# A Mamba-2 layer with a small mixture of experts: dt's logarithm in PSUM, sums of squares by transposes, six banks and new prices in the planner

## The chip, the core and the metric

The kernel runs on one core of a Trainium2 chip. TensorE (PE) multiplies, VectorE (DVE), ScalarE (ACT) and GpSimd (POOL) work on the elements, and SyncE (SP) issues the DMAs. The metric is the time on the device in microseconds (us) for one launch; less is better. All data are fp32.

## The reference

A sequence of 1024 tokens with 512 features is normalised (layernorm without weights). Two branches take the result, and both are added to the input.

The first is a Mamba-2 layer with 128 heads of 64 channels, state size 128, 8 groups, and chunks of 128 tokens:

```python
proj = einsum('bsd,ed->bse', x, in_proj_w)       # 18560 rows: gate 8192, hBC 10240, dt 128
hBC = silu(conv1d(hBC, width 4, per channel) + conv_b)
hs, B, C = split(hBC)                            # 8192, 8 x 128, 8 x 128
dt = clip(softplus(dt + dt_bias), 0, 100)
A_dt = dt * -exp(A_log);  A_cum = cumsum over a chunk
Y_diag = C B^T * exp(segsum(A_dt)) @ (hs * dt)   # inside a chunk
states = B^T @ (hs * dt * exp(A_last - A_cum))   # handed from chunk to chunk
Y_off = C @ previous state * exp(A_cum)
y = (Y_diag + Y_off + hs * D) * silu(gate)
out = rmsnorm in 8 groups of 1024 (y) * norm_w @ out_proj_w.T
```

The second is a linear layer of 512 x 512 plus LoRA experts of rank 16: softmax over 8 experts, the best two, weights renormalised, scaled by 2.

## The kernel before

**Precision.** A wide product of fp32 matrices is made of three products of fp32r halves: high x high, high x low, low x high. ScalarE rounds the high half, POOL (or VectorE) subtracts to get the low half (`split`, L311). Some products (y, yo, cb, the old sums of squares) are plain fp32 and appear as two records each in the trace.

**The start.** x is loaded in eight blocks, normalised, transposed on TensorE (xT) and split into XH and XL (L352 to L391). The dt rows are projected first (pp_dt, two halves of 512 tokens, L407). Softplus is relu(v) + log(1 + exp(-|v|)): ScalarE writes |v| to `dtu` and relu(v) to `dtv` in SBUF, then the exponential in place in `dtu`; VectorE evaluates a polynomial of degree 10 for the logarithm (L433 to L438: one scaling and nine multiply-adds per half), adds, clips, multiplies by A and scans (`ac`, L445). `dtv`, `ac` and the decay are transposed (tt_dt, tt_As, tt_dec). The router and the FFN (`ffn`, L482) run in between; the FFN's products are pf0 to pf7.

**The middle.** For each unit u of 4 heads (32 units): two blocks of the gate and two of hs are projected by `block` (L639, 12 products of 512 columns per half, bank pp_r), hs goes through the convolution (ScalarE the first tap, VectorE three, L658 and L667) and silu; hs is transposed (hT, L749) and multiplied by dt (xdt); decay gives xf, split into xdh and xdl (L757 to L766); 21 products ps of 256 columns make the chunk states (L775), which VectorE chains (st, L782 to L787); yo (L808) is the part from earlier chunks, y (L819) the part inside a chunk, with the matrix L that ScalarE (L731, L733) and VectorE (L735) build from a broadcast load of A_cum. VectorE evacuates them (tt L811, yt L823), POOL adds and multiplies by the gate (L826, L829), and the result is stored in DRAM (g_d). Every fourth unit, `group` projects B and C and makes cb (L679).

**The end.** For each group g of 1024 channels and each block z of 128 tokens, the gated values come back (gr), are split into gh and gl, and are multiplied by the split output weights (po, 24 products of 512 columns, L891). For the norm, ScalarE squares in place, VectorE sums over the eight channel blocks (sq, L883), and TensorE sums over the partitions: a product of sq with a column of ones gives one number per token (vp, L902), for two blocks z at a time. ScalarE takes the root (L904), VectorE the reciprocal, and po times it is added to acc (L910). With the last group acc is stored.

**What sets the order.** The program's instructions are recorded as `op`s with an engine, a planned duration, an urgency and the buffers they take. `Plan.run` (L123) then replays planned times and, whenever an engine is free, takes the ready op with the smallest urgency whose buffers are there. The resulting order is fixed in each engine's queue; at run time semaphores alone decide when an instruction starts. PSUM is a pool of 8 banks, and `BANKS` caps how many of each kind may live: mm (wide accumulators, also bt and cb), ts (transposes, ps, vp) and yy (y and yo). An op that is marked `long` is of the wide sort on TensorE:

```python
                    if o.table and o.table != table:
                        urge += URGE["switch"]
                    if e == "PE" and o.long != long:
                        urge += URGE["turn"]
```

A wide op after one that isn't long also costs `TURN` in the plan (L196 to L199). ps isn't marked long here.

## Time and profile before

| | |
|---|---|
| median of 3 runs (lowest to highest) | 1666.13 us (1664.14 to 1667.02) |
| profiled execution, its own time | 1664.26 us |
| its span, first to last instruction | 1662.5 us |
| mean granted TensorE clock | 0.997 |
| busy share of PE, DVE, ACT, POOL | 98%, 78%, 76%, 53% |
| ACT table loads | 176 |
| wide projections pp_r | 3456 products |
| output projection po | 1536 products |
| y, yo, ps, hT records | 2048, 896, 672, 512 |
| vp records | 128, 16.3 us busy |

In the lines shown below, a row of the timeline reads: start and length in us, engine, line of the kernel, operation, output and inputs (buffer numbers left out), shapes, how many were merged, and in brackets the idle time before it and what ended it. A row of the table of stretches reads: from and to, length, then busy us and count of instructions for PE, PEld (weight loads), DVE, ACT and POOL, the granted TensorE clock, the DMA share and GB/s. A row of a tile's page under "its engine sat idle before it" names who ended the wait, the us in total and how many times. Rows of neighbouring products overlap, since a product's length includes its way through the array; the distance between two starts is what one product costs.

### The profile page before, as it was taken

The page shows a single profiled execution, that of the slowest core. Times are in us where ns is not written, and L with a number is a line of the kernel's source. Part 1 is how long each engine was busy: PE and PEld are TensorE (multiplying, and loading weights), DVE is VectorE, ACT ScalarE, POOL GpSimd, SP SyncE. Part 2 cuts the span into 40 slices and gives each one's busy share as a digit, 9 for nine tenths or more (in the row PEclk, how much of TensorE's full clock was granted, in tenths as well). Part 3 has the DMA queues.
Part 4 walks back from the last instruction along what each step waited for, and adds up shares of the span by engine and source line. Part 5 has one row for each costly group of instructions (what it writes and reads, how often), then busy time and mean ns, then how long its engine had stood idle before and what let it go on. Part 6 is the DMA issues. An engine that isn't in the chain of part 4 may idle for free.

```text
span 1662.5 us, 27030 instructions
## 1 busy us (share of the span) xinstructions
PE 1635.5 (98%) x9732; PEld 1363.3 (82%) x9732; DVE 1298.8 (78%) x2205; ACT 1268.0 (76%) x2262; POOL 881.2 (53%) x769
## 2 busy tenths in 40 slices
PE   7999999999999999999999999999999999999998
PEld 5688888888888888888888888888887788888887
DVE  7249978878787888787777878877779987787774
ACT  4836999897998889899979979898999444444441
POOL 4017866875866687677758766875776300000000
PEclk9999999999999999999999999999999999999999
DMA  4542644534444355344434444545454755544522
GB/s 140 178 145 76 194 134 141 172 127 149 132 129 148 113 157 164 130 130 162 143 118 144 128 136 129 174 143 158 128 175 143 212 152 152 137 124 122 151 67 72
DMA packets 142903, 234.07 MB, mean 141 GB/s; under 512 B 11312, under 2 KB 76976, under 8 KB 142768
## 3 DMA queue, kind: packets, MB, share of 16 engines
q1 hardware_dynamic: 142768, 232.33, 45.6%
q8 instruction: 77, 1.26, 0.3%
q14 instruction: 58, 0.48, 0.1%
HBM read 193.49 MB, written 38.80 MB: 140 GB/s over the span
## 4 chain that ended last, share of the span: by engine, by line
PE 80%; DVE 5%; ACT 3%; issue 2%; POOL 1%; DMA 1%; SPq 0%; DVEq 0%; ACTq 0%; POOLq 0%
PE pp_r L401 38%; PE po L891 20%; PE y L819 6%; PE yo L808 6%; PE ps L775 5%; PE hT L749 3%; DVE h L667 2%; DVE L L735 1%; PE cb L705 1%; DVE owl L866 1%; PE vp L902 1%; ACT g L651 1%; POOL xdl L764 1%; ACT xdh L762 1%; DVE sq L883 0%
## 5 line engine op out<-in xcount | busy, mean ns | idle before, releaser
L401 PE MATMUL pp_r<-xh,wh 128*128 128x512 f32 x1152 | 465.2, 404 | 0.0
L401 PE MATMUL pp_r<-xl,wh 128*128 128x512 f32 x1152 | 450.8, 391 | 0.0
L401 PE MATMUL pp_r<-xh,wl 128*128 128x512 f32 x1152 | 450.8, 391 | 0.0
L731 ACT ACTIVATE L<-L,As 128x128 f32<-128x128 f32 x1024 | 316.6, 391 | 0.9 <-DMA L<-acum_d 0.8
L667 DVE SCALAR_TENSOR_TENSOR h<-pp_r,cw,h 128x512 f32<-128x512 f32 (+2 forms) x384 | 287.2, 748 | 36.5 <-ACT h L658 27.5
L313 POOL TENSOR_TENSOR wl<-wr,wh 128x512 fp32r<-128x512 f32 x144 | 187.3, 1310 | 169.3 <-ACT wh L312 157.2
L826 POOL TENSOR_TENSOR yt<-yt,tt 128x384 f32<-128x384 f32 (+1 forms) x128 | 180.2, 1410 | 153.6 <-DVE tt L811 92.8
L401 PEld LDWEIGHTS pp_r<-xh,wh 128*128 128x128 f32 x1152 | 217.1, 188 | 46.7 <-issue 6.2
L401 PEld LDWEIGHTS pp_r<-xh,wl 128*128 128x128 f32 x1152 | 216.5, 188 | 47.2
L401 PEld LDWEIGHTS pp_r<-xl,wh 128*128 128x128 f32 x1152 | 217.3, 189 | 40.2 <-issue 0.2
L735 DVE TENSOR_TENSOR L<-L,cbm 128x1024 f32<-128x1024 f32 x128 | 189.5, 1487 | 35.3 <-ACT L L733 34.9
L829 POOL TENSOR_TENSOR g<-yt,g 128x512 f32<-128x512 f32 x128 | 181.7, 1422 | 5.8
L764 POOL TENSOR_TENSOR xdl<-xf,xdh 128x512 fp32r<-128x512 f32 (+1 forms) x128 | 149.6, 1187 | 56.2 <-ACT xdh L762 56.2
L757 POOL TENSOR_TENSOR xf<-xdt,dec 128x512 f32<-128x512 f32 (+1 forms) x128 | 152.6, 1208 | 37.2 <-DVE xdt L751 37.1
L786 DVE SCALAR_TENSOR_TENSOR st<-st,eA,ps 128x64 f32<-128x64 f32 x768 | 150.3, 275 | 1.1
L883 DVE TENSOR_REDUCE sq<-gr 128x128 f32<-128x1024 f32 x64 | 128.4, 2007 | 18.0 <-ACT gr L882 17.2
L658 ACT ACTIVATE h<-pp_r,cb,cw 128x512 f32<-128x512 f32 (+1 forms) x128 | 98.5, 770 | 57.5 <-PE pp_r L401 56.9
L819 PE MATMUL y<-L,xdt 128*64 128x128 f32 x2048 | 135.6, 278 | 1.6 <-DVE L L735 1.0
L733 ACT ACTIVATE L<-L 128x1024 f32<-128x1024 f32 x128 | 135.4, 1058 | 1.4
L819 PEld LDWEIGHTS y<-L,xdt 128*64 128x64 f32 x2048 | 110.0, 136 | 28.3 <-issue 9.4
L891 PE MATMUL po<-owh,gh 128*128 128x512 f32 x512 | 131.8, 397 | 0.0
L882 ACT ACTIVATE gr<-gr 128x1024 f32<-128x1024 f32 x64 | 67.7, 1058 | 80.8 <-DVE gl L880 80.3
(174 smaller groups left out, 2809.3 us busy)
## 6 DMA issues: line engine op xcount, KB each, us to landing
L<-acum_d SPq DMA_DIRECT2D x128, 512.0 KB, 5.7
wr<-in_w SPq DMA_DIRECT2D x144, 256.0 KB, 3.0
g_d<-g SPq DMA_DIRECT2D x64, 512.0 KB, 3.0
gr<-g_d SPq DMA_DIRECT2D x64, 512.0 KB, 6.9
e<-exp_d SPq DMA_DIRECT2D x128, 224.0 KB, 4.5
ow<-out_w SPq DMA_DIRECT2D x64, 256.0 KB, 3.1
x<-x SPq DMA_DIRECT2D x8, 256.0 KB, 4.7
xa<-x SPq DMA_DIRECT2D x8, 256.0 KB, 3.2
```

Of the source, the lines that this page charges most:

```text
L313: op("POOL", dur[1], lambda: pool.tensor_tensor(lo(), raw(), f32(hi()), ALU.subtract), r=[raw, hi], w=[lo], urge=urge, port=True)
L401: pe.matmul(acc(), a[:, k, :], b[:, k, halves(half)], start=n == 0, stop=n == 11)
L667: dve.scalar_tensor_tensor(d, acc()[:, :n], cw[:, ci, k:k + 1], d, ALU.mult, ALU.add)
L731: act.activation(L()[:, z, :], L()[:, z, :], AF.Relu, bias=As()[:, z, h:h + 1], scale=-1.0)
L735: op("DVE", 1.14, lambda L=L: dve.tensor_tensor(L(), L(), gr.cbm(), ALU.mult), r=[gr.cbm], w=[L], urge=at("Lm") + 0.05 * a, port=True)
L757: op("POOL", 1.0 if n == 4 else 0.8, lambda xf=xf, j=j, b=b, zs=zs, n=n: pool.tensor_tensor(xf().rearrange("p z (a c) -> p z a c", a=2), x ...
L764: op("POOL", 1.24 if n == 4 else 0.96, lambda xf=xf, zs=zs, cols=cols: pool.tensor_tensor(xdl()[:, zs, cols], xf(), f32(xdh()[:, zs, cols] ...
L786: dve.scalar_tensor_tensor(st()[:, z, c], st()[:, z - 1, c], eA()[:, 4 * u + a, z:z + 1], pt()[:, z % 2, c], ALU.mult, ALU.add)
L819: pe.matmul(yp()[64 * a:64 * a + 64, zsl(z4)], xdt[j]()[:, z, 64 * a:64 * a + 64], M[2 * j + a]()[:, z, :], start=True, stop=True)
L826: op("POOL", 1.3 if n == 4 else 1.0, lambda yt=yt, tt=tt, part=part: pool.tensor_tensor(yt()[:, part], yt()[:, part], tt()[:, part], ALU.a ...
L829: op("POOL", 1.3, lambda yt=yt, j=j, hf=hf: pool.tensor_tensor(gate[j]()[:, halves(hf)], yt(), gate[j]()[:, halves(hf)], ALU.mult), r=[yt] ...
L891: pe.matmul(po(), a()[:, b, :], wts[g, b // per][k]()[:, b % per, :], start=n == 0, stop=n == 23)
```

## The change

- **dt.** The exponential stays in PSUM: ScalarE writes |v| and then exp(-|v|) in place into the accumulator pp_dt, and VectorE's polynomial reads it there. Its instructions are no longer planned on the SBUF port shared with POOL (`port=True` goes), so the plan doesn't keep them apart from POOL's.
- **Sums of squares.** sq of four blocks z (two in the last group) share one tile. TensorE transposes each of them (128 columns, one record) into one bank, and VectorE reduces along the tokens' rows in PSUM; then the root on ScalarE and the reciprocal for all four at once. Four po accumulators wait for it instead of two.
- **Banks.** mm may hold six banks instead of five.
- **Prices.** Going from wide to narrow on TensorE costs an urgency of 0.065, from narrow to wide 0.135 (before 0.018 both ways), and `TURN` is 0.13 instead of 0.09. ps counts as long. Most other urgencies have new values.
- **Loads.** The planned landing times of the eight loads of x differ, and the dt weights are loaded after the sixth instead of the fourth. Some planned durations are new.

```diff
--- before.py
+++ after.py
@@ -41,7 +41,8 @@
 SWITCH = 1.3
-TURN = 0.09
-URGE = dict(w=-0.906, part=-0.044, proj=0, evac=-0.05, silu=0, group=-0.136, hT=0.273, xdt=0.663, xf=1.191,
-            split=0.55, ps=0.69, st=0.536, Ll=0.1, Lr=1.008, Le=0.296, Lm=1.16, el=0.3, yo=0.952, tt=0.642, y=0.92,
-            yt=0.737, out=0.8, switch=0.3, turn=0.018, c0=32.2, c=0.022, ffn=-3.656, early=-3.5, w0=31)
-BANKS = dict(mm=5, ts=3, yy=3)
+TURN = 0.13
+URGE = dict(w=-0.813, part=-0.179, proj=0, evac=0.099, silu=-0.096, group=-0.136, hT=0.272, xdt=0.765, xf=1.065,
+            split=0.327, ps=0.69, st=0.495, Ll=0.114, Lr=1.681, Le=0.456, Lm=1.16, el=0.441, yo=1.177, tt=0.256,
+            y=1.1, yt=0.811, out=0.8, switch=0.345, short=0.065, long=0.135, c0=32.207, c=0.032, ffn=-2.955,
+            early=-3.189, w0=31)
+BANKS = dict(mm=6, ts=3, yy=3)
 
@@ -151,3 +152,3 @@
                     if e == "PE" and o.long != long:
-                        urge += URGE["turn"]
+                        urge += URGE["short" if long else "long"]
                     if best is not None and (best_urge, best.n) <= (urge, o.n):
@@ -248,4 +249,2 @@
                        channel_multiplier=-1)
-    ones = ctile([P, 1], "ones")
-    pool.memset(ones, 1.0)
     eps_t = ctile([P, 1], "eps_t")
@@ -277,3 +276,3 @@
     K |= {n: Kind(small, c) for n, c in dict(wr=3, wh=3, wl=3, y=2, tt=2, xf=2).items()}
-    K |= {n: Kind(small, c, late=True) for n, c in dict(acc=8, sq=3, ow_r=4).items()}
+    K |= {n: Kind(small, c, late=True) for n, c in dict(acc=8, sq=2, ow_r=4).items()}
     banks = Pool("banks", 8, HALF, psum)
@@ -333,7 +332,8 @@
         for i in range(2):
-            dma(lambda xt=xt, i=i: xt()[:, i, :], lambda z=2 * j + i: x[zsl(z), :], 3.0, w=[(xt, 1 << i)],
+            dma(lambda xt=xt, i=i: xt()[:, i, :], lambda z=2 * j + i: x[zsl(z), :],
+                (2.7, 2.9, 4.3, 4.6, 4.8, 5.0, 5.3, 5.5)[2 * j + i], w=[(xt, 1 << i)],
                 urge=-8.0 + 0.01 * j)
         xts.append(xt)
-        if j == 1:
-            dma(wdt[0], lambda: in_w[144], 3.0, w=[wdt[0]], urge=-7.985)
+        if j == 2:
+            dma(wdt[0], lambda: in_w[144], 5.2, w=[wdt[0]], urge=-7.975)
 
@@ -368,6 +368,6 @@
         for i in range(2):
-            op("DVE", 0.8, stats(i), r=[(xt, 1 << i)], w=[(sc, 1 << i)], urge=ur)
+            op("DVE", 0.87, stats(i), r=[(xt, 1 << i)], w=[(sc, 1 << i)], urge=ur)
         op("ACT", 0.2, lambda mv=mv, rs=rs: act.activation(rs, mv[:, 1:4:2], AF.Sqrt, bias=eps_t), r=[sc], w=[sc],
            urge=ur, table="sqrt")
-        op("DVE", 0.25, scales, r=[sc], w=[sc], urge=ur)
+        op("DVE", 0.36, scales, r=[sc], w=[sc], urge=ur)
         op("POOL", 0.77, lambda xn=xn, xt=xt, rs=rs, nm=nm: pool.tensor_scalar(
@@ -406,3 +406,4 @@
 
-    dtv, dtu, ac, eT = (new("e", n) for n in ("dt_v", "dt_u", "acum", "eT"))
+    dtv, ac, dtu, eT = (new("e", n) for n in ("dt_v", "acum", "dt_u", "eT"))
+    us = []
     for half in range(2):
@@ -410,6 +411,6 @@
         project(wdt[1:], acc, half, -6.0)
-        op("ACT", 0.57, lambda acc=acc, h=half: act.activation(dtu()[:, halves(h)], acc(), AF.Abs, bias=dtb),
-           r=[acc, CONST], w=[(dtu, zmask(half))], urge=-6.0)
         op("ACT", 0.57, lambda acc=acc, h=half: act.activation(dtv()[:, halves(h)], acc(), AF.Relu, bias=dtb),
            r=[acc, CONST], w=[(dtv, zmask(half))], urge=-6.0)
+        op("ACT", 0.57, lambda acc=acc: act.activation(acc(), acc(), AF.Abs, bias=dtb), r=[CONST], w=[acc], urge=-6.0)
+        us.append(acc)
     reset, q = new("L", "reset", P), new("L", "dt_q")
@@ -430,10 +431,9 @@
         mk = zmask(half)
-        op("ACT", 0.52, lambda hv=hv: act.activation(dtu()[:, hv], dtu()[:, hv], AF.Exp, scale=-1.0), w=[(dtu, mk)],
-           urge=-5.9, table="exp")
-        op("DVE", 0.35, lambda hv=hv: dve.tensor_scalar(q()[:, hv], dtu()[:, hv], LOG1P[-1], None, ALU.mult),
-           r=[(dtu, mk)], w=[(q, mk)], urge=-5.8, port=True)
+        u = us[half]
+        op("ACT", 0.5, lambda u=u: act.activation(u(), u(), AF.Exp, scale=-1.0), w=[u], urge=-5.9, table="exp")
+        op("DVE", 0.62, lambda hv=hv, u=u: dve.tensor_scalar(q()[:, hv], u(), LOG1P[-1], None, ALU.mult),
+           r=[u], w=[(q, mk)], urge=-5.8)
         for c in LOG1P[-2::-1]:
-            op("DVE", 0.6, lambda c=c, hv=hv: dve.scalar_tensor_tensor(q()[:, hv], q()[:, hv], c, dtu()[:, hv], ALU.add,
-                                                                       ALU.mult), r=[(dtu, mk)], w=[(q, mk)], urge=-5.8,
-               port=True)
+            op("DVE", 0.66, lambda c=c, hv=hv, u=u: dve.scalar_tensor_tensor(q()[:, hv], q()[:, hv], c, u(), ALU.add,
+                                                                             ALU.mult), r=[u], w=[(q, mk)], urge=-5.8)
         op("DVE", 0.6, lambda hv=hv: dve.tensor_tensor(dtv()[:, hv], dtv()[:, hv], q()[:, hv], ALU.add), r=[(q, mk)],
@@ -776,3 +776,3 @@
             op("PE", 0.36 * len(zz), products, r=[(gr.bh, mk & 255), (gr.bl, mk & 255), (xdh, mk), (xdl, mk)], w=[pt],
-               urge=at("ps") + 0.02 * i, take=[st] if not i else ())
+               urge=at("ps") + 0.02 * i, take=[st] if not i else (), long=True)
 
@@ -849,3 +849,3 @@
     wts = {}
-    crs = ctile([P, 64], "crs")
+    crs = ctile([P, 72], "crs")
     for g in range(G):
@@ -868,3 +868,3 @@
                 r=[raw, (hi, 1 << b % per), CONST], w=[(lo, 1 << b % per)], urge=urge, port=True)
-        sqs, pos = {}, {}
+        pos, many = {}, 4 if g < G - 1 else 2
         for z in range(NZ):
@@ -874,3 +874,4 @@
             raw, gh, gl = new("gr", f"gr{g}_{z}", P), new("gh", f"gh{g}_{z}", P, FR), new("gl", f"gl{g}_{z}", P, FR)
-            sq = new("sq", f"sq{g}_{z}", shape=[P, P])
+            if z % many == 0:
+                sq = new("sq", f"sq{g}_{z}", P)
             dma(raw, lambda g=g, z=z: g_d[g][:, :, zsl(z)].rearrange("b p t -> p b t"), 5.9, r=[G_D[g]], w=[raw],
@@ -882,4 +883,5 @@
             op("ACT", 0.97, lambda raw=raw: act.activation(raw(), raw(), AF.Square), w=[raw], urge=urge)
-            op("DVE", 1.93, lambda raw=raw, sq=sq: dve.tensor_reduce(sq(), raw().rearrange("p b t -> p t b"), AX.X,
-                                                                     ALU.add), r=[raw], w=[sq], urge=urge)
+            op("DVE", 1.93, lambda raw=raw, sq=sq, at=z % many: dve.tensor_reduce(
+                sq()[:, at, :], raw().rearrange("p b t -> p t b"), AX.X, ALU.add), r=[raw], w=[(sq, 1 << z % many)],
+                urge=urge)
             po = new("mm", f"po{g}_{z}")
@@ -893,18 +895,20 @@
                    urge=urge + URGE["c"], long=True)
-            sqs[z], pos[z] = sq, po
-            if z % 2:
-                vp = new("ts", f"vp{g}_{z}")
-                rs = crs[:, 2 * (g * 4 + z // 2):2 * (g * 4 + z // 2) + 2]
+            pos[z] = po
+            if z % many == many - 1:
+                vp = new("ts", f"vp{g}_{z}", P)
+                first = z - many + 1
+                rs = crs[:, g * NZ + first:g * NZ + z + 1]
                 RS = thing(f"rs{g}_{z}")
 
-                def sums(vp=vp, pair=(sqs[z - 1], sqs[z])):
-                    for j, s in enumerate(pair):
-                        pe.matmul(vp()[:, j:j + 1], s(), ones, start=True, stop=True)
-                op("PE", 0.42, sums, r=[sqs[z - 1], sqs[z]], w=[vp], urge=urge + URGE["c"] - 0.1)
-                op("ACT", 0.25, lambda vp=vp, rs=rs: act.activation(rs, vp()[:, 0:2], AF.Sqrt, bias=eps_t,
-                                                                    scale=1.0 / 1024.0), r=[vp], w=[RS], urge=urge,
-                   table="sqrt")
+                def sums(vp=vp, sq=sq, many=many):
+                    for j in range(many):
+                        pe.transpose(vp()[:, j, :], sq()[:, j, :], ident)
+                op("PE", 0.115 * many, sums, r=[sq], w=[vp], urge=urge + URGE["c"] - 0.1)
+                op("DVE", 0.1 + 0.13 * many, lambda vp=vp, rs=rs, many=many: dve.tensor_reduce(
+                    rs, vp()[:, 0:many, :], AX.X, ALU.add), r=[vp], w=[RS], urge=urge)
+                op("ACT", 0.25, lambda rs=rs: act.activation(rs, rs, AF.Sqrt, bias=eps_t, scale=1.0 / 1024.0), w=[RS],
+                   urge=urge, table="sqrt")
                 op("DVE", 0.2, lambda rs=rs: dve.reciprocal(rs, rs), w=[RS], urge=urge)
-                for j in range(2):
-                    zz = z - 1 + j
+                for j in range(many):
+                    zz = first + j
                     op("DVE", 0.67, lambda zz=zz, j=j, rs=rs, p=pos[zz]: dve.scalar_tensor_tensor(
```

## The prediction, made before the result was known

> **What bounds the kernel.** I read the page first: busy time by engine.
> ```profile
> PE 1635.5 (98%) x9732; PEld 1363.3 (82%) x9732; DVE 1298.8 (78%) x2205; ACT 1268.0 (76%) x2262; POOL 881.2 (53%) x769
> ```
> TensorE is busy for 98% of the span, so time can only come from its products, from the distance between them, or from the 27 us that are left. A busy row hides the distance, since the rows of neighbouring products overlap. So next I read TensorE's instructions in order of time, and took starts, not durations.
> ```profile
> 315.85 0.39 PE L401 MATMUL pp_r<-xl,wh 128*128 128x512 f32 x1
> 316.08 0.39 PE L401 MATMUL pp_r<-xh,wl 128*128 128x512 f32 x1
> 316.31 1.05 PE L808 MATMUL yo<-C,st 128*128 128x128 f32 x8
> 317.29 1.09 PE L819 MATMUL y<-L,xdt 128*64 128x128 f32 x16
> 318.31 1.83 PE L808 MATMUL yo<-C,st 128*128 128x128 f32 x14
> 319.90 0.47 PE L401 MATMUL pp_r<-xh,wh 128*128 128x512 f32 x1
> 320.21 0.39 PE L401 MATMUL pp_r<-xl,wh 128*128 128x512 f32 x1
> ...
> 321.13 0.40 PE L401 MATMUL pp_r<-xh,wl 128*128 128x512 f32 x1
> 321.46 1.09 PE L819 MATMUL y<-L,xdt 128*64 128x128 f32 x16
> 322.48 0.50 PE L401 MATMUL pp_r<-xh,wh 128*128 128x512 f32 x1
> 322.82 0.40 PE L401 MATMUL pp_r<-xl,wh 128*128 128x512 f32 x1
> ...
> 339.52 1.97 PE L819 MATMUL y<-L,xdt 128*64 128x128 f32 x32
> 341.42 0.39 PE L775 MATMUL ps<-xdh,bh 128*128 128x256 f32 x1
> ...
> 1384.88 0.50 PE L902 MATMUL vp<-ones,sq 128*128 128x1 f32 x4
> 1385.24 1.65 PE L891 MATMUL po<-owh,gh 128*128 128x512 f32 x6
> ```
> In a steady stream two wide (512-column) products start 0.227 us apart. After yo or hT the first two wide ones are 0.31 apart (319.90 to 320.21), after y 0.34. A product enters y 0.09 late (321.13 to 321.46), and sixteen y products take 1.02 to the next start, while 32 in one run take 1.90: the second sixteen cost 0.88. So a change of sort has a price, and the order of the products matters.
>
> Third, the stretches of the beginning, and what ends TensorE's longest wait there.
> ```profile
> 34.30:41.10 6.80, 0.00 (x0) 0.01 (x1) 6.80 (x13) 0.00 (x0) 0.00 (x0) 0.79 0.00 0
> 41.10:48.50 7.40, 5.82 (x19) 4.79 (x20) 5.39 (x16) 3.22 (x5) 0.00 (x0) 0.50 0.01 2
> ```
> ```profile
> 24.00 3.37 DVE L436 SCALAR_TENSOR_TENSOR dt_q<-dt_q,dt_u 128x512 f32<-128x512 f32 x2
> 106.78 2.33 DVE L667 SCALAR_TENSOR_TENSOR B<-pp_r,cw,B 128x512 f32<-128x512 f32 x3 [5.96 <-ACT B L658]
> ...
> 41.12 1.09 PE L459 MATMUL tt_dt<-ident,dt_v 128*128 128x128 f32 x4 [6.85 <-DVE dt_v L441]
> ```
> TensorE does nothing from 34.3 to 41.1 while VectorE works through dt's logarithm, and the granted clock then reads 0.50 up to 48.5. Last, whom the state products (ps) wait for:
> ```profile
>   POOL xdl L764: 12.8, 25
> ```
>
> The profiled execution took 1664.26 us (span 1662.5, 1.76 around it). The median of the runs is 1666.13, so I carry the sum on 1664.3 and call the 1.9 between them noise; 0.2% (3.3 us) is about what a measurement can tell from no change.
>
> **Sums of squares.** Before, 32 visits of four one-column records (two products, two records each). Measured from the last wide start before a visit to the fourth wide start after it, less the wide gaps themselves, a visit costs 0.474 us: four gaps of 0.11 and a slow return. After, 14 visits of four transposes and 4 of two. hT, the same kind of transpose, has the same gap, 0.109, so a visit of four is taken at 0.474 and one of two at 0.25: 15.2 falls to 7.6, **-7.6**. Here the Trainium skill speaks against the change: TensorE: Matmul & The Clock Gate, section "Wait — 56ns, not 53.3ns?", lets a product's distance follow its columns, about 56 ns at 128 columns, with a floor of 25 ns for tiny ones. As an estimate from that page, 128 records at 25 ns, 3.2 us, would become 64 at 56 ns, 3.6 us: a loss of 0.4. The trace's 0.11 for one column decides otherwise.
> New on VectorE are 18 reductions of at most 128x512 from PSUM, about 0.7 each by the xa row (0.69), 12 us over the last 375, where VectorE idles 20 in each 100 (1400 to 1600); 14 fewer reciprocals and 14 fewer roots go. All lies beside TensorE: taken at 0, ends 0 and +3, since the very first sum now needs four squares, 8 us of VectorE, instead of two, in a stretch (1280 to 1300) where TensorE already loses 4.3 us to VectorE's queue. The last group sums two at a time, so the tail (one accumulate, 0.75, and a store) stays.
>
> **Order of the products.** I counted the neighbours in TensorE's built order of both programs; the products are otherwise the same. Runs of y: 104 become 80. Each boundary costs 0.10 at the exit and 0.09 at the entry: 24 x 0.19 = -4.6. Returns from y to wide products: 30 become 10, at 0.14 each (0.114 on the first gap, 0.027 on the next three): -2.8. Returns from hT and yo: 127 become 70, at 0.107: -6.1; but such an exit itself takes 0.03 where one inside narrow work takes 0.11, so the 57 lost exits give back 4.6. Returns from ps: 24 become 48, at 0.02: +0.5. Sum -8.4. Multiplying every gap of both orders by its median gives -17.0 for this and the sums of squares together, against 16.0 by hand (the rest is small mixed neighbours): I take **-17.0**. It is the firmest term, since the counts are exact.
>
> **Waits of ps.** From a unit's last hT product to its first ps product lie 6.6 us of products at the median before, 12.8 after, while the chain between (xdt 0.68, xf 1.2, xdh 0.6, xdl 1.2, twice through POOL) is the same. Of the 12.8 us of idle, 9 should go; ends 0 and -12.8. **-9.** Late next would be yo behind VectorE's state steps.
>
> **The banks.** Six for mm leave fewer for the rest. In the order of banks, a y or yo tile's bank is taken again within 4 us of its last product once before, 34 times after (within 6 us: 14, then 67). VectorE's evacuation ends 2.1 us after y's last product started at the median, 3.8 at the third quartile, 4.5 at the ninth decile. A wait on such a bank stands in TensorE's queue ahead of everything. At the median none waits; some will: **+4**, ends 0 and +27 (34 waits of 0.8, everything as late as the third quartile).
>
> **ScalarE's tables.** 176 loads become 197, 21 x 1.28 = 27 us more on an engine at 90% in the middle. Counted from start to start, its work in one group was 125 of 150.6 us (423.5 to 574); three more loads make 129 of about 148: covered by ScalarE's own waits for pp_r (57 us in all), 0; if that cover is gone, part of the 27.
>
> **The beginning.** The weights of dt move behind two more loads of x (two SP issues, 0.9 us); split on ScalarE (0.63) and POOL (1.27, behind one xn) they are ready by about 11, needed at 12.8: 0. One more weight load stands before the store of acum, but its buffer is free by about 47 and acum not before 48: 0. The logarithm now reads PSUM: the x3 row from PSUM steps 0.79 (2.33 less 0.75, halved); the SBUF step alone is 0.60, but 1.7 while POOL runs (24.00, two in 3.37), and the PSUM rows show no such stretching (733 to 751 ns). More important, VectorE now finishes the first half before the second. From 22.9: 14 steps of 0.79, then 1.7 for the rest, gives dt_v at 35.6, not 40.9. TensorE meanwhile has six more products and is at 34.4: a wait of 1.4 instead of 6.85. Then acum needs until 39.0 (wait 0.5), the router's weights until 45.7 (wait 2.2), decay until 53.9 (wait 1), and the first FFN product starts at 58.4 instead of 64.5 with 12 more wide products (2.7) behind it: 8.8, of which the half clock is about 2.5. **-9**, ends -5 (as if the clock dropped anyway) and -11 (PSUM steps of 0.67). Against it stands the Trainium skill, VectorE: DVE Perf Modes, "Rules for kernel authors": copy from PSUM first where many operations follow. By it, with SBUF steps of 0.60 and the new order, dt_v would come 2.7 us sooner than I reckon; the row at 24.00 says what POOL makes of that.
>
> **Sum.** 1664.3 - 17.0 - 9 + 4 - 9 = 1633.3; with some of the runs' spread, 1634.
>
> **Rivals.** (1) The order gains but the waits do not: ps keeps its idle time, the banks cost 15, the beginning brings 5: 1664.3 - 17 + 15 - 5 = 1657. For it: 34 short returns of banks; against: VectorE already waits for y 20 times (19.7 us), so it is often early. (2) Slower: VectorE becomes late on the narrow banks. It needs more than 38.3 us (35 gained, 3.3 to be seen): at 34 tight banks 1.1 us each. With the ninth decile's 4.5 us of evacuation against about 3.2 of room, 34 x 1.3 = 44, so 1673. Against it: that decile would have to be the rule. (3) The beginning is hidden anyway, or the clock falls in another place, the rest as forecast: 1642. (4) ScalarE's loads come onto the path in full: 1633.3 + 27 = 1660.
>
> **How the numbers follow.** Forecast (1624 to 1642, with rival 3 in it) 0.70; rival 1 0.12; rival 4 0.06; rival 2 0.07; no visible change 0.05. The low end takes ps whole, no bank wait, 11 at the beginning: 1664.3 - 17 - 12.8 - 11 = 1623.5. The high end reaches to rival 1. Faster 0.88, same 0.04, slower 0.08.
>
> **What would show it.** Right: about 150 distances from narrow to wide products; the wait for xdl under 4 us; no stretch with clock 0.50 after 20 us; the first FFN product near 58; a group of four units every 148 us, not 150.6. Wrong: idle before y or yo products released by VectorE's tt or yt, over 15 us in all; ScalarE without waits for pp_r; an idle stretch of over 4 us in the first 60.

## The result, and the profile after

The changed kernel takes 1658.71 us (median of 6 runs, 1656.57 to 1659.25), beside 1666.58 us for the kernel before (6 runs). The ratio is 0.9957, 95% interval 0.9947 to 0.9968: 7.9 us faster in the medians. Forecast were 32, so the sign was right, the size was not, and the time lies above the range. The profiled execution took 1658.2 us (span 1656.5), 6.1 less than the one of before.

The page of the changed kernel, busy time by engine (us, share, instructions) and then the chain that ended last, as shares by engine:
```profile
PE 1623.1 (98%) x9668; PEld 1360.7 (82%) x9668; DVE 1293.4 (78%) x2209; ACT 1290.1 (78%) x2269; POOL 879.0 (53%) x768
...
PE 43%; ACT 22%; DVE 21%; POOL 7%; issue 5%; DMA 2%; SPq 0%; DVEq 0%; ACTq 0%; POOLq 0%
```
The chain of the kernel before:
```profile
PE 80%; DVE 5%; ACT 3%; issue 2%; POOL 1%; DMA 1%; SPq 0%; DVEq 0%; ACTq 0%; POOLq 0%
```
TensorE is still busy for 98%, but the chain now stands on it for 43% of the span (80% before); on ScalarE and VectorE it stands for 43% between them (8% before). The work that TensorE needs comes off their queues just in time, or late. To see where, I cut both traces at the same four places: the first ps of unit 0, the first ps of unit 28, the start of the second output group, the start of the last product. "Counted" is the sum over TensorE's built order of the median distance of each pair of neighbours, all medians from the trace of before; what a stretch takes beyond it is called waiting. It depends on how finely the neighbours are sorted: other sortings of the same trace give -4 to -7 us where the table has -3.6, and 13 to 16 us of added waiting in the middle where it has 12.6. So the split is good to about 3 us; the lengths themselves are read directly.

| us | before | after | forecast for the difference | measured |
|---|---|---|---|---|
| start to first ps | 140.7 | 132.6 | -9 | -8.1 |
| middle, ps of unit 0 to ps of unit 28 | 1035.9 | 1044.9 | -8.6 (counted -3.6, waits of ps -9, banks +4) | +9.0 |
| of it counted | 1015.6 | 1012.0 | -3.6 | -3.6 |
| passage, from there to the second output group | 163.2 | 163.5 | -6.0 (all counted) | +0.3 |
| second output group to the last product | 318.2 | 311.2 | -7.3 (all counted) | -7.0 |

Start and end came near the forecast. The whole miss of 25 us lies in the middle (17.6) and in the passage (6.3). From the third group of four units on, a group takes 151.3 to 151.7 us, where 148 was forecast and 150.6 to 150.7 stood before.

Here is one of eight like places in the middle of the changed kernel, the first product of y in unit 19. TensorE, in order of time (start, us, product, idle before it and what ended it):
```profile
473.95 0.43 PE L819 MATMUL y<-L,xdt 128*64 128x128 f32 x2
475.01 1.96 PE L819 MATMUL y<-L,xdt 128*64 128x128 f32 x30 [0.62 <-DVE L L735]
```
And VectorE's queue up to that point, in the same columns:
```profile
443.26 1.23 DVE L735 TENSOR_TENSOR L<-L,cbm 128x1024 f32<-128x1024 f32 x1
449.90 1.48 DVE L735 TENSOR_TENSOR L<-L,cbm 128x1024 f32<-128x1024 f32 x1 [5.42 <-ACT L L733]
455.58 4.68 DVE L667 SCALAR_TENSOR_TENSOR h<-pp_r,cw,h 128x512 f32<-128x512 f32 x6 [4.20 <-ACT h L658]
460.18 0.41 DVE L782 COPY st<-ps 128x256 f32<-128x256 f32 x1
460.63 4.69 DVE L786 SCALAR_TENSOR_TENSOR st<-st,eA,ps 128x64 f32<-128x64 f32 x24
465.23 2.32 DVE L667 SCALAR_TENSOR_TENSOR h<-pp_r,cw,h 128x512 f32<-128x512 f32 x3
...
470.31 2.31 DVE L667 SCALAR_TENSOR_TENSOR h<-pp_r,cw,h 128x510 f32<-128x510 f32 x3
472.54 1.28 DVE L751 TENSOR_TENSOR xdt<-hT,dts 128x512 f32<-128x512 f32 x2
473.74 3.21 DVE L735 TENSOR_TENSOR L<-L,cbm 128x1024 f32<-128x1024 f32 x2
```
VectorE first stands still twice, 5.42 and 4.20 us, each time for ScalarE. The order of its queue is fixed, so nothing behind passes. Then it has some 19 us of work without a gap, and the L that TensorE wants stands at the end of it. A busy share of 78% over the span says nothing of this.

VectorE's waits over the whole execution, before (releaser; us, times, longest):
```profile
...
DVE xdt L751 <- PE hT L749: 54.9, 27, 2.4
DVE st L782 <- PE ps L775: 44.2, 19, 3.0
DVE L L735 <- ACT L L733: 34.9, 28, 2.3
DVE h L667 <- ACT h L658: 27.5, 30, 1.6
...
DVE yt L823 <- PE y L819: 19.7, 20, 1.6
...
DVE B L667 <- ACT B L658: 17.0, 10, 7.4
```
and after:
```profile
DVE L L735 <- ACT L L733: 130.2, 30, 6.8
DVE h L667 <- ACT h L658: 45.6, 27, 4.2
DVE B L667 <- ACT B L658: 42.7, 9, 7.0
...
DVE yt L823 <- PE y L819: 4.4, 7, 2.4
...
DVE xdt L751 <- PE hT L749: 2.8, 4, 1.5
```
Before, VectorE's idle time in the middle was in good part waiting for TensorE (xdt, st, yt): it was early, and had slack where it mattered. After, it waits for ScalarE, in few long pieces, and hardly for TensorE (xdt 2.8, yt 4.4, no row for st). TensorE's own longest sums of waits after, first as the rows of TensorE give them, then the row for xdl under the tile ps, which adds the weight loads:
```profile
PE ps L775 <- POOL xdl L764: 8.1, 15, 2.2
PE y L819 <- DVE L L735: 4.4, 8, 0.6
PE xT L385 <- ACT xn L376: 3.9, 1, 3.9
```
```profile
  POOL xdl L764: 20.1, 35
```
The wait for xdl, 12.8 us before and forecast under 4, is 20.1. In distances beyond the counted ones the middle has 9.7 us inside ps (7.8 before) and 12.4 inside y (6.4 before); the rest of the 12.6 us that the middle waits longer, some 5 us, lies at hT and cb.

### The profile page after: what moved, and what is told of

Same layout as the page of the kernel before. It is cut to its first block, busy times and chain, and to the rows that moved or that the text cites. A ratio compares the mean times of both kernels' runs of the same rounds, so it can differ in the third digit from the quotient of the medians.

```text
span 1656.5 us, 26998 instructions
## 1 busy us (share of the span) xinstructions
PE 1623.1 (98%) x9668; PEld 1360.7 (82%) x9668; DVE 1293.4 (78%) x2209; ACT 1290.1 (78%) x2269; POOL 879.0 (53%) x768
## 4 chain that ended last, share of the span: by engine, by line
PE 43%; ACT 22%; DVE 21%; POOL 7%; issue 5%; DMA 2%; SPq 0%; DVEq 0%; ACTq 0%; POOLq 0%
PE po L893 20%; PE pp_r L401 12%; ACT L L731 6%; DVE h L667 5%; DVE st L786 3%; ACT L733 3%; PE y L819 3%; ACT L L733 2%; DVE L L735 2%; PE yo L808 2%; PE ps L775 2%; ACT g L651 2%; DVE yt L823 2%; DVE tt L811 2%; DVE B L667 2%
## 5 line engine op out<-in xcount | busy, mean ns | idle before, releaser
L401 PE MATMUL pp_r<-xh,wh 128*128 128x512 f32 x1152 | 457.5, 397 | 0.0
L312 POOL TENSOR_TENSOR wl<-wr,wh 128x512 fp32r<-128x512 f32 x144 | 204.1, 1423 | 219.2 <-ACT wh L311 147.4
L735 DVE TENSOR_TENSOR L<-L,cbm 128x1024 f32<-128x1024 f32 x128 | 191.3, 1502 | 130.3 <-ACT L L733 130.2
L826 POOL TENSOR_TENSOR yt<-yt,tt 128x384 f32<-128x384 f32 (+1 forms) x128 | 161.1, 1267 | 136.5 <-DVE tt L811 117.3
L829 POOL TENSOR_TENSOR g<-yt,g 128x512 f32<-128x512 f32 x128 | 191.1, 1500 | 4.5
L764 POOL TENSOR_TENSOR xdl<-xf,xdh 128x512 fp32r<-128x512 f32 (+1 forms) x128 | 161.9, 1276 | 28.9 <-ACT xdh L762 28.0
L757 POOL TENSOR_TENSOR xf<-xdt,dec 128x512 f32<-128x512 f32 (+1 forms) x128 | 137.1, 1084 | 4.7 <-DVE xdt L751 4.7
L893 PE MATMUL po<-owh,gl 128*128 128x512 f32 x512 | 126.5, 389 | 0.0
```

The source lines that it names most:

```text
L312: op("POOL", dur[1], lambda: pool.tensor_tensor(lo(), raw(), f32(hi()), ALU.subtract), r=[raw, hi], w=[lo], urge=urge, port=True)
L401: pe.matmul(acc(), a[:, k, :], b[:, k, halves(half)], start=n == 0, stop=n == 11)
L735: op("DVE", 1.14, lambda L=L: dve.tensor_tensor(L(), L(), gr.cbm(), ALU.mult), r=[gr.cbm], w=[L], urge=at("Lm") + 0.05 * a, port=True)
L764: op("POOL", 1.24 if n == 4 else 0.96, lambda xf=xf, zs=zs, cols=cols: pool.tensor_tensor(xdl()[:, zs, cols], xf(), f32(xdh()[:, zs, cols] ...
L826: op("POOL", 1.3 if n == 4 else 1.0, lambda yt=yt, tt=tt, part=part: pool.tensor_tensor(yt()[:, part], yt()[:, part], tt()[:, part], ALU.a ...
L829: op("POOL", 1.3, lambda yt=yt, j=j, hf=hf: pool.tensor_tensor(gate[j]()[:, halves(hf)], yt(), gate[j]()[:, halves(hf)], ALU.mult), r=[yt] ...
```

## The experiments

First the changes apart, then the cause. All times stand beside runs of the kernel before on the same chip (medians 1665.3 to 1666.6). "One run" is a single run with a profile. The stages are those of the table above; the waits of the middle are its length less what is counted for the order of that kernel. Kernels with the same order there repeat the middle to 0.5 us (1035.9 to 1036.4 in five traces, 1044.9 to 1045.3 in four), so single runs can be compared by it. The expectation of sums_only counts the last stage 1 us longer than this table, before and after.

| kernel | time, us | start | middle | waits in it | passage | end |
|---|---|---|---|---|---|---|
| before | 1666.6 | 140.7 | 1035.9 | 20.3 | 163.2 | 318.2 |
| changed | 1658.7 | 132.6 | 1044.9 | 32.9 | 163.5 | 311.2 |
| no_prices | 1648.1 | 136.8 | 1036.4 | 20.9 | 159.6 | 311.3 |
| prices_only | 1673.6 | 141.8 | 1045.3 | 33.3 | 162.4 | 318.6 |
| dt_only | 1659.0 | 135.2 | 1035.9 | 20.4 | 163.3 | 318.2 |
| sums_only | 1655.4 | 140.8 | 1035.9 | 20.3 | 159.6 | 311.3 |
| no_prices_oldx | 1644.4 | 131.8 | 1036.0 | 20.4 | 159.6 | 311.3 |
| after_oldx | 1656.3 | 131.7 | 1044.9 | 33.0 | 162.5 | 311.2 |
| after_mm5, one run | 1657.9 | 132.3 | 1045.0 | 33.0 | 163.4 | 311.2 |
| before_exp, one run | 1653.9 | 140.7 | 1027.5 | 11.9 | 161.1 | 318.2 |
| after_exp, one run | 1647.2 | 135.2 | 1033.5 | 21.5 | 161.0 | 311.2 |
| after_light, one run | 1649.4 | 132.8 | 1037.5 | 25.5 | 161.6 | 311.3 |
| before_taps, one run | 1656.6 | 142.0 | 1027.9 | 12.3 | 162.1 | 318.2 |
| after_taps, one run | 1630.8 | 133.7 | 1020.6 | 8.6 | 159.2 | 311.2 |
| after_Lhalf, one run | 1644.3 | 133.7 | 1034.8 | 22.9 | 158.5 | 311.3 |
| before_both, one run | 1653.4 | 141.1 | 1026.5 | 10.9 | 161.2 | 318.2 |
| after_both, one run | 1630.4 | 132.5 | 1020.4 | 8.4 | 160.3 | 311.2 |
| aox_poolB | 1658.6 | 134.0 | 1040.9 | 31.2 | 170.3 | 311.1 |
| aox_poolA, one run | 1666.6 | 138.7 | 1040.4 | 28.9 | 170.3 | 311.2 |
| oldx_poolB, one run | 1648.9 | 130.8 | 1039.1 | 21.1 | 161.7 | 311.3 |

**The new prices taken out** (no_prices): dt in PSUM and the sums by transposes stay, the planner's prices, the mark on ps and the banks go back.
```diff
-TURN = 0.13
-URGE = dict(w=-0.813, part=-0.179, ...
+TURN = 0.09
+URGE = dict(w=-0.906, part=-0.044, ...     # all of the kernel before
-BANKS = dict(mm=6, ts=3, yy=3)
+BANKS = dict(mm=5, ts=3, yy=3)
-                        urge += URGE["short" if long else "long"]
+                        urge += URGE["turn"]
-            op("PE", 0.36 * len(zz), products, ..., long=True)
+            op("PE", 0.36 * len(zz), products, ...)
```


> The changed kernel with the old urgencies, the old TURN, five mm banks and ps not long: dt in PSUM, the new loads of x and the sums of squares by transposes stay. Theory A: the new prices' order of the middle is what lost; it saves 1.0 us of products per group but adds 3 table loads (3.9 us of ScalarE) per group and makes the chain to ps late. Then this kernel has the middle of before (150.6 us per group) and keeps the gains at the start (about -8) and at the end (about -8): 1664.3 - 16 = 1648 to 1651. Rival B: the middle is slower for a reason that doesn't hang on the prices (the changed start, the memory of the tiles): then it stays near 1658. Rival C: the six banks and the longer chains are what paid: over 1660.

Measured: 1648.11 us, ratio 0.9892 (0.9875 to 0.9909), 10.6 us faster than the changed kernel. The middle is back at 1036.4.

**The new prices alone** (prices_only): the same lines, the other way round, put into the kernel before.

> The kernel before with the new urgencies, TURN, six mm banks and ps long, and nothing else. Theory A: a group of four units takes 151.5 us instead of 150.6, waits of products in the middle 10 us above before, with the passage to the output projection some us later: 1664.3 + 8 = 1670 to 1675. By my forecast (products' order -8.4, ps waits -9, banks +4) it would be 1651. Rival B: no more than 2 us from before.

Measured: 1673.56 us, ratio 1.0046 (1.0031 to 1.0061): slower. Its middle, 1045.3 with 33.3 of waits, is that of the changed kernel. So the change has two halves of opposite sign, and all that was lost in the middle belongs to the order that the prices make.

**Is it ScalarE's table loads?** (after_exp, before_exp): each Silu becomes an exponential, so that 3 loads are left of 197 and of 176.
```diff
-            op("ACT", 0.97, lambda: act.activation(dst(), dst(), AF.Silu), ...
+            op("ACT", 0.97, lambda: act.activation(dst(), dst(), AF.Exp), ...
```
The planner's table names stay, so that TensorE's order does not move.

> The changed kernel with every silu computed as an exponential, so that ScalarE loads no table in the middle (3 loads instead of 197); the order of all other instructions is the same, and the output is not the layer's. Theory A (ScalarE's queue with its loads makes xdh, L and so ps and y late): a group falls from 151.5 to 147 to 148.5 us, near the sum of its gaps (146.8), and the wait of ps for xdl from 20 to under 5 us; whole about 1632 to 1638. Rival D (POOL's own queue, stretched to 2.3 us an instruction beside VectorE, or banks taken again too early): the waits stay over 12 us and the group over 150.

> The same in the kernel before (3 loads instead of 176). Theory A: a group falls from 150.6 to about 148.5 to 149.5 (sum of gaps 147.8), so without loads the changed kernel is faster by about 1 us per group and by some 20 us in all, as forecast; whole about 1652. Rival D: both fall by as much as each other or not at all, and the changed group stays above this one.

Measured: 1647.16, between the two theories, and 1653.87. In the middle the loads cost the kernel before 8.4 us and the changed one 11.4. That 21 more loads cost all their 27 us is out; 3 of the 12.6 us of new waits may be theirs. Without any of them the changed middle is still 6.0 us the longer one. The wait for xdl falls in both, but y's 12.4 stays (12.5): ScalarE's loads alone do not explain it.

**Each other half alone** (dt_only, sums_only), to see whether the gains add up.
```diff
 # dt_only: the hunks of the change on x's loads, the norm's stated times, dt_u, dt_q; nothing else
 # sums_only: the hunks on sq, vp, crs; nothing else
```


> Only the part with dt is put into the kernel before: dt's exponential in PSUM, the new stated arrival times of x and the new stated times of the norm. TensorE's order behind the first FFN product is that of before. Theory A (the parts add up: the version without the new prices was 17.5 us faster than before, 9 of it counted at the end of the kernel and some 4 at its start): only the start gains, by 2 to 6 us as it did in the version without prices (first FFN product at 63.4 or sooner, start of the first ps near 136.8 instead of 140.7), and nothing follows in the middle: 1660 to 1664. Theory B (a gain at the start is given back behind it, since the middle waits for VectorE, ScalarE and POOL and not for TensorE): the first ps is earlier, but the last product stands within 1 us of before: 1665 to 1667.

> Only the sums of squares by transposes are put into the kernel before. Theory A (the distances of products counted in the prediction, minus 7.6 us, and nothing new waits): 1656 to 1659, the stretch from the second output group to the end 312 us long instead of 319, and the middle unchanged at 1036. Theory B (the reductions on VectorE delay something in the output projection or in the middle): 1660 to 1666, with a middle over 1038 or an end over 315.

Measured: dt_only 1658.99 (ratio 0.9953, 0.9936 to 0.9969), sums_only 1655.42 (0.9934, 0.9919 to 0.9948). Both gained a little more than expected; 7.0 and 10.6 add up to 17.6, and the two together (no_prices) gained 17.2. The start's 5.5 us were still there at the end: nothing behind it took them back.

**The stated arrival of x put back** (no_prices_oldx, after_oldx):
```diff
-            dma(..., (2.7, 2.9, 4.3, 4.6, 4.8, 5.0, 5.3, 5.5)[2 * j + i], ...
+            dma(..., 3.0, ...
-        if j == 2:
-            dma(wdt[0], lambda: in_w[144], 5.2, ...
+        if j == 1:
+            dma(wdt[0], lambda: in_w[144], 3.0, ...
-            op("DVE", 0.87, stats(i), ...         -        op("DVE", 0.36, scales, ...
+            op("DVE", 0.8, stats(i), ...          +        op("DVE", 0.25, scales, ...
```


> The version without the new prices, and with the stated arrival times of x and stated times of the norm put back to those of before; dt's exponential in PSUM and the sums by transposes stay. Theory A (the new stated times put VectorE's normalizing steps in an order in which TensorE idles 4 us at 9 to 13 us and then runs at half clock for 7 us): without them no half clock between 14 and 21 us, the first FFN product at 58 to 61 instead of 63.4, and 1643 to 1646 in all. Theory B (the idle time comes from the arrival of x, whatever the stated times; or the clock falls all the same): half clock at the same place or another within the first 60 us, 1647 to 1650.

> The changed kernel with the stated arrival times of x and the stated times of the norm put back to those of before. Theory A (they cost the same 3 to 4 us here as without the new prices, all of it ahead of the first group of units): 1654 to 1656.5, the first ps at 128 to 130 instead of 132.6, the middle 1044 to 1046 as in the changed kernel. Theory B (what is gained at the start is given back behind it, or the start doesn't gain here): 1657 to 1660.

Measured: no_prices_oldx 1644.40 (1643.48 to 1645.11), ratio 0.9868 (0.9853 to 0.9882). It is the fastest whole layer of this study, 22 us under the kernel before and 14 under the changed one. Against no_prices it is 3.7 us lower in the medians, but the intervals overlap a little. The reason that I gave holds in half: the 4 us of idle time at 9 us are gone, but the clock fell all the same, at 10.3 instead of 14.5, and only a second fall at 52 us is missing. after_oldx, 1656.27 (ratio 0.9949, 0.9933 to 0.9966), can't be told from the changed kernel, and its first ps came at 131.7, not at 128 to 130.

**Whose queue?** after_light relieves ScalarE in the changed kernel:
```diff
-                    for z in range(hf * 4, hf * 4 + 4):
-                        act.activation(L()[:, z, :], L()[:, z, :], AF.Relu, bias=As()[:, z, h:h + 1], scale=-1.0)
+                    for z in (hf * 4, hf * 4 + 2):
+                        act.activation(L()[:, z:z + 2, :], L()[:, z:z + 2, :], AF.Relu, bias=As()[:, z, h:h + 1], scale=-1.0)
```


> The changed kernel, in its own order on TensorE and VectorE and with all table loads, but ScalarE's Relu on L takes two token tiles at once (2 instructions for a half of L instead of 4; both tiles take the first one's bias, so the output is not the layer's). That frees about 0.9 us of ScalarE for each of the 128 L, some 14 us of the 151 us of a group of four units. Theory A (the new order makes y and ps wait because their chains stand in ScalarE's queue): y's waits for L and the waits for xdl fall by more than half, the middle from 1045 to 1024 to 1033, groups at 148 to 149.5, 1636 to 1647 in all. Theory B (they wait for VectorE's and POOL's own queues, or for banks): the middle stays above 1040, 1653 to 1658 in all.

after_taps relieves VectorE instead, after_both both, before_both and before_taps are the counterparts:
```diff
-                for k in range(1, 4):
+                for k in range(2, 4):
                     j = 3 - k
```


> The changed kernel in its own order, with one of the three taps left out that VectorE adds in the convolution of h, B and C (the output is not the layer's). That takes 0.75 us from VectorE in front of many of its other steps, some 90 us of its 1293 in all; ScalarE is left as it is. Theory A (TensorE's waits at the first product of y are waits for VectorE's own queue: in the 13 us before such a product VectorE did not stand still, and the product of L with cb was its last step): the eight waits of 0.7 to 1 us at y go, y's sum in the middle falls from 12.4 to some 5, the waits of ps for xdl stay near 8 to 10, the middle is 1036 to 1040 long and the whole 1647 to 1652. Theory B (L is late because the exponential is, on ScalarE): y's sum stays above 10, the middle above 1042.

> The changed kernel in its own order with both engines relieved: ScalarE's Relu on L two token tiles at once, VectorE's convolution with two taps (the output is not the layer's). Theory A (the waits that the new order added in the middle stand in the queues of ScalarE and VectorE, and the distances that it saves are there once the queues are free): middle 1022 to 1030, 1012 counted and 10 to 18 of waits, the whole 1632 to 1643. Theory B (they come from banks, or from the chain of products itself): middle above 1034.

> The kernel before with the same two reliefs, as the counterpart (the output is not the layer's). Theory A (with free queues only the counted distances of TensorE are left, 1015.6 in the middle against the changed kernel's 1012.0): middle 1024 to 1030, 2 to 5 us longer than the changed kernel's, and from the first output group to the second the same sign. Theory B (the order before is the better one even with free queues): middle shorter than the changed kernel's.

> The kernel before with two of three taps (the output is not the layer's), ScalarE as it was. Theory A (the order before leaves VectorE room, so its relief brings little; what its middle lost was ScalarE's table loads): middle 1028 to 1034 against 1036, 1656 to 1662 in all. Theory B (the relief brings every order as much): middle below 1016, 1640 or less.

The page of after_light, of after_taps and of after_both, busy time by engine; TensorE's instructions are the same 9668 in the same order:
```profile
PE 1619.1 (98%) x9668; PEld 1360.2 (83%) x9668; DVE 1303.2 (79%) x2209; ACT 1201.2 (73%) x1757; POOL 882.1 (54%) x768
```
```profile
PE 1610.4 (99%) x9668; PEld 1357.3 (83%) x9668; DVE 1199.2 (74%) x2049; ACT 1291.5 (79%) x2269; POOL 874.4 (54%) x768
```
```profile
PE 1610.3 (99%) x9668; PEld 1357.3 (83%) x9668; DVE 1201.1 (74%) x2049; ACT 1204.1 (74%) x1757; POOL 879.0 (54%) x768
```
89 us off ScalarE bring 9.3 us of time; 94 us off VectorE bring 27.9; both together bring no more than VectorE's alone. TensorE's waits in after_light:
```profile
PE y L819 <- DVE L L735: 4.5, 5, 1.2
...
PE ps L775 <- POOL xdl L764: 3.9, 6, 2.1
```
and in after_taps, where the row for y and L is gone and that for ps is a single wait in the passage:
```profile
PE ps L775 <- POOL xdl L764: 1.8, 1, 1.8
PE y L819 <- issue: 1.7, 1, 1.7
```
With ScalarE relieved the time came out between the two theories: ps's waits in the middle fell from 9.7 to 4.0, as the one had it, and y's stayed (13.3), as the other had it. With VectorE relieved y's fell to 3.4 (before_taps has 4.6) and ps's to 0.2, and the time came out 16 us below the expected range. The fall of ps's waits I had not expected: I had put them down to ScalarE and POOL, but the chain to xdl begins with VectorE's xdt. The waits of the middle come to 8.6 us. VectorE's long stands for L are still there in after_taps (125.0 us, against 130.2); the work that stands behind them is shorter.

The counterpart settles the worth of the order. The same tap left out of the kernel before gives 1656.56, its middle fell by 8.0 against 24.3. With VectorE relieved in both, the changed kernel's middle is 7.3 us shorter than that of before (1020.6 against 1027.9) and its whole time 25.8; with both engines relieved it is 6.1 and 23.0. In those kernels the forecast's gain of 31 is mostly there. So what the new order saves is real, and waits that less work on VectorE removes take it back. No run puts TensorE's new order beside the old orders of the other engines, so whether VectorE is late because its own work was moved, or because TensorE now asks for its results in another order, is not shown.

**Queue or tap?** The tap also frees the accumulators and lets Silu start sooner. after_Lhalf takes a like amount from VectorE at another step:
```diff
-lambda L=L: dve.tensor_tensor(L(), L(), gr.cbm(), ALU.mult)
+lambda L=L: dve.tensor_tensor(L()[:, 0:4, :], L()[:, 0:4, :], gr.cbm()[:, 0:4, :], ALU.mult)
```


> The changed kernel in its own order, with all three taps, but VectorE multiplies only the first four token tiles of each L with cb (the output is not the layer's). That takes some 0.6 us from each of 128 products, about 75 us of VectorE in all, against 90 with the tap left out. Theory A (VectorE's queue as such held up y and, by xdt, the chain to ps): middle 1020 to 1028, 1630 to 1641 in all, y's sum near 4 to 6 and the waits of ps under 4. Theory B (the tap mattered because the accumulators come free and ScalarE's Silu starts sooner, not because of the queue): middle above 1036, only y's own waits shorter.

Measured: 1644.29, middle 1034.8, between the two theories. Its row against that of the changed kernel's 1502 ns:
```profile
L735 DVE TENSOR_TENSOR L<-L,cbm 128x512 f32<-128x512 f32 x128 | 125.5, 988 | 141.8 <-ACT L L733 141.8
```
Half the elements saved 0.51 us each, 66 us in all and not 75. y's waits fell from 12.4 to 7.5 and ps's from 9.7 to 6.2, 10 us of the middle against 24 by the tap. So VectorE's queue is part of the cause wherever it is shortened, but it matters where. ScalarE's waits show one difference. At Silu it waits for VectorE's convolution, in the changed kernel:
```profile
ACT h L670 <- DVE h L667: 58.2, 30, 5.2
...
ACT L670 <- DVE h L667: 11.9, 10, 2.4
```
That is 70 us, where the kernel before has 20. With the tap left out it is 31, with half of L it is still 60. The two queues wait for each other, VectorE for L and ScalarE for h, and of the two reliefs the tap shortens ScalarE's side by far the more. How the other 14 us divide between this and the 94 against 66 us taken off VectorE stays open.

**Is it the banks?** after_mm5: `BANKS = dict(mm=5, ts=3, yy=3)` in the changed kernel.

> The changed kernel with five accumulator banks instead of six, the instructions of TensorE in the same order. Theory A (the planner did not need the sixth bank, the waits come from the queues): the same within 3 us, 1655 to 1662. Theory B (the sixth bank carries the longer runs of narrow products, or takes a bank that y and yo miss): 1664 or more with new waits of the projections for their banks, or 1652 or less.

Measured: 1657.92, every stage within 0.3 us. The sixth bank neither helped nor hurt this order.

**A relief that leaves the layer whole** (aox_poolB, aox_poolA, oldx_poolB): some of the products of L with cb go to POOL.
```diff
-            op("DVE", 1.14, lambda L=L: dve.tensor_tensor(L(), L(), gr.cbm(), ALU.mult), ...
+            eng, e, d = ("POOL", pool, 2.45) if a == 3 and u % 2 else ("DVE", dve, 1.14)    # aox_poolA: a == 3
+            op(eng, d, lambda L=L, e=e: e.tensor_tensor(L(), L(), gr.cbm(), ALU.mult), ...
```


> The version with the old stated times of x and the new prices, and one in eight of the products of L with cb (16 of 128) on POOL instead of VectorE; the layer is whole. That takes 16 times 1.5 us, 24 us, from VectorE and puts some 16 times 2.5 us on POOL, which was busy for 745 of 1035 us in the middle. Theory A (VectorE's queue holds back y's L and, by xdt, the chain to ps): middle 1028 to 1038 instead of 1045, 1637 to 1650 in all. Theory B (POOL stands in the same chain with xf and xdl, and pays the gain back): middle 1040 to 1050, 1650 to 1660.

> The same with one in four of the products of L with cb (32 of 128) on POOL: 48 us less on VectorE, some 80 us more on POOL. Theory A (VectorE's queue alone): middle 1022 to 1034, shorter than with one in eight. Theory B (POOL pays it back): middle longer than with one in eight, 1040 or more, with waits of ps for xdl above 12 us.

> The version without the new prices, with the old stated times of x, and one in eight of the products of L with cb on POOL; the layer is whole. Its middle waits for VectorE less than that of the new prices (y's sum 6.4 us against 12.4, and with both reliefs the middle of before fell by 9 against 25). Theory A: middle 1030 to 1036 against 1036, 1639 to 1645 in all, no more than 6 us from the relief. Theory B (POOL pays it back): middle above 1038, 1646 or more.

Measured: 1658.58 (ratio 0.9962, 0.9948 to 0.9977), 1666.59, 1648.94; none beats the version that it started from (after_oldx for the first two, no_prices_oldx for the third). With one in four on POOL y's waits do fall, from 12.2 to 3.8 us, but ps's rise from 9.8 to 12.8, and the start grows by 7 and the passage by 8. POOL stands in the chain to xdl itself. The planner also makes a new order of each of these, so they show the sum and not POOL's price alone.

## Why the prediction was wrong

**What failed.** Two steps, both about waits.

"Waits of ps": I saw that the distance in products between a unit's last hT and its first ps grows from 6.6 to 12.8 us, took the chain between as "the same", and booked 9 us. The chain was not the same. For a quarter of a unit, from the first of its four transposes hT to the end of its xdl, it took 7.8 us at the median before and 15.8 after: xdt now starts 3.2 us after its transposes instead of 0.2 (VectorE's queue), and xf 7.3 us after xdt instead of 0.9 (POOL's queue, with yt, g and wl put in front; yt in turn stands for VectorE's tt, 117.3 us in all against 92.8). The chain grew with the distance. The wait for xdl rose by 7 us where I had it fall by 9. Nor was all of the 12.8 us there to be had: it includes the weight loads' waits, and only 7.8 us of it stretched the distances in the middle. In distances the term came to +1.9 where -9 was booked.

The second is an omission. I costed the new order for TensorE alone, and let everything that the planner moved on VectorE and ScalarE lie beside it. No term stood for y waiting for L, nor for new waits in the passage. They measured +6.0 in the middle for y and some 5 for hT and cb. With ps's 10.9 and less the 4 that were booked for the banks, that makes the 17.6 of the middle. The passage missed by 6.3; the first ps of the last unit and the first y of the last block wait longest there. TensorE there in the changed kernel, in order of time:
```profile
1276.07 1.97 PE L819 MATMUL y<-L,xdt 128*64 128x128 f32 x32
1279.99 0.39 PE L775 MATMUL ps<-xdh,bh 128*128 128x256 f32 x1 [1.95 <-ACT xdh L762]
1280.21 0.28 PE L775 MATMUL ps<-xdh,bl 128*128 128x256 f32 x1
1282.71 0.58 PE L775 MATMUL ps<-xdl,bh 128*128 128x256 f32 x1 [2.23 <-POOL xdl L764]
...
1303.61 2.62 PE L819 MATMUL y<-L,xdt 128*64 128x128 f32 x29 [2.00 <-issue]
```
These idle times are not all of it. The granted clock falls to half behind them, for 10.2 us in the passage, and does not fall there before. As an estimate from the trace, the products inside those stretches stand 3.7 us further apart in sum than their medians, the long idle times not counted.

The signs were in reach: the order of VectorE was built like that of TensorE, and I had counted only TensorE's neighbours. I had noted ScalarE at 90% in the middle, which left the chain through it little room for a new order.

**What held.** The counted distances: -16.9 us in the three stages of the table, and where VectorE was relieved in both (after_taps against before_taps) the gain showed. The sums of squares: 7.6 forecast, 10.6 measured alone (8.7 to 13.5 by its interval), so the sign held and the size was a little short. The gain agrees with the trace's 0.11 us a product. The Trainium skill, TensorE: Matmul & The Clock Gate, section "Wait — 56ns, not 53.3ns?", has a floor of 25 ns for tiny products. Taken as their price it made the prediction's estimate a loss of 0.4; the run decides against that. The reductions on VectorE cost nothing that can be seen. The beginning, forecast -9, came to -8.1 at the first ps, in part by luck: with the same new dt it was -5.5 in dt_only and -3.9 in no_prices, whose products have one order there and whose clock fell at different times. The logarithm's step from PSUM, forecast 0.79, took 0.72 in a row of eight:
```profile
26.20 5.75 DVE L437 SCALAR_TENSOR_TENSOR dt_q<-dt_q,pp_dt 128x512 f32<-128x512 f32 x8
...
36.30 0.42 DVE L441 TENSOR_SCALAR dt_v<-dt_v 128x512 f32<-128x512 f32 x1
```
dt_v's first half is ready at 36.7 (forecast 35.6), and the 6.85 us of idle time are gone. But 3.9 us of idle time are new, at 9 us, where the transposes of x wait for the norm's xn on ScalarE (4.4 us in no_prices, 1.9 with the old stated times in no_prices_oldx), and the first FFN product starts at 60.3, not 58.4.

**ScalarE's tables**, taken at 0: 0 to 3. **The banks**, taken at +4: 0, as no wait of y or yo for tt or yt is among TensorE's rows.

**The rivals.** Nearest is the first, 1657, in which ps keeps its idle time; but its other 15 us were to come from banks and came from VectorE and the passage, so its number is met by chance. The second had VectorE late, and VectorE was late, on L and xdt and not on banks; the whole miss was 25 us instead of 44. The third is out, since the start's gain stayed. The fourth, 1660, is as near in time as the first, but by after_exp and before_exp the 21 loads cost 3 us at most and not 27.

**The signs that were named.** Of those for the forecast, the count of distances from narrow to wide products held (154, before 222), which is the built order and says nothing of waits. The wait for xdl under 4 us, a group every 148 us, no half clock after 20 us and the first FFN product near 58 all failed. Of those against it, none came: no wait for tt or yt of 15 us, ScalarE still waiting for pp_r, no idle stretch over 4 us (3.9 at most). The list against had no line for what happened.

## What to carry to other kernels

A planner that is told new prices for one engine rewrites the order of all of them. Count what it did to the in-order queues that feed that engine, above all where one of them now waits long for another and what work is then stacked behind, before booking the distances saved. More products between two ends of a chain are room only if the chain has not grown by as much. And a change of several parts is worth taking apart: here two parts gained 17 us together, and the third gave 8 of them back when measured alone and 11 beside the others.

## What the hardware showed that was not expected

The granted clock falls for less idle time than I had thought, and at new places. In the changed kernel it was at half from 14.2 to 21.1 us, from 1280.6 to 1287.4 and from 1304.5 to 1307.9. Its stretches last 3.41 us or a multiple of it, so I cut the trace of the changed kernel on that grid (stretch, its length, PE's busy time, then the granted clock, DMA share, GB/s):
```profile
10.81:14.23 3.42, 1.09 (x8) 1.00 0.70 240
14.23:17.64 3.41, 2.31 (x5) 0.50 0.95 291
...
1277.16:1280.57 3.41, 1.38 (x19) 1.00 0.89 296
1280.57:1283.98 3.41, 1.27 (x6) 0.50 0.88 279
...
1301.05:1304.47 3.42, 1.42 (x19) 1.00 0.60 207
1304.47:1307.88 3.41, 3.41 (x26) 0.50 0.02 7
```
Each fall follows a stretch in which TensorE was busy for 1.1 to 1.4 us of 3.4, with a single idle time of only 2 us in the two late ones. Busy time does not decide it alone: a stretch with 1.57 us, at 7.4 in the same trace, was followed by full clock, and in no_prices one with 3.32, at 48.6, by half (it held eight transposes and products with weights of 8 rows, and wide products only at its start). What half clock makes of the same product is seen in ps, 0.21 us apart at 1283 and 0.11 apart at 1287.6:
```profile
1283.31 0.42 PE L775 MATMUL ps<-xdh,bl 128*128 128x256 f32 x1
1283.52 0.41 PE L775 MATMUL ps<-xdl,bh 128*128 128x256 f32 x1
...
1287.62 0.28 PE L775 MATMUL ps<-xdh,bl 128*128 128x256 f32 x1
1287.73 0.28 PE L775 MATMUL ps<-xdl,bh 128*128 128x256 f32 x1
```
Where it falls is in part chance. after_mm5 has the changed kernel's products in the same order, and its half clock stood at 12.9 to 19.7, 1282.7 to 1286.1 and 1303.1 to 1306.6. no_prices and dt_only have one order of products up to 1280 us, and there it stood at 14.5 to 21.3 and 52.0 to 58.9 in the first, at 11.4 to 21.7 and 52.4 to 55.8 in the second. In every trace here, the stretches that an execution's end did not cut off last 3.4, 6.8, 10.2 or 13.7 us. The Trainium skill, TensorE: Matmul & The Clock Gate, section "What's actually happening", has a window of about 3.4 us that runs freely and does not start with the kernel. The lengths and the changing places here fit it. The same section lets the clock fall after an idle window. Here 2 us without products in a window were enough.
